# Six products of one tap instead of seven taps in five products, in a chain of filters on one Trainium2 core

## The chip, the cores and the metric

One core of one Trainium2 chip. TensorE (PE) multiplies, with its weight loads shown apart (PEld); VectorE (DVE), ScalarE (ACT) and GpSimd (POOL) work beside it; SyncE (SP) issues DMAs. The metric is device time of one launch in microseconds, here the median of three runs.

## The reference

The input x is 128 signals of 64 channels and 1024 samples, with a style vector of 128 numbers for each signal. Four convolution layers of three taps follow each other, and the result is added to x:

```python
s = style @ mw.T + mb
weight = SCALE * w * s[:, None, :, None]
demod = lax.rsqrt(jnp.sum(weight * weight, axis=(2, 3)) + EPS)
weight = weight * demod[:, :, None, None]
...
'same':       out = conv_same(x, weight) + b
'upsample':   out = blur(conv_up(x, weight) + b, 2 * [1, 3, 3, 1] / 8)
'downsample': out = conv_down(blur(x, [1, 3, 3, 1] / 8), weight) + b
...
x + layer3(layer2(layer1(layer0(x))))      # same, upsample, same, downsample
```

No nonlinear function stands between the layers, so the four of them are, for one signal, a single linear filter. The kernel forms that filter and applies it.

## The kernel before

Signals are taken four at a time, in 32 groups q. On the 128 partitions lie two halves of 64 channels (T and Bo), and every product of 64x64 is four matmuls, one for each quadrant of TensorE (`HALF` by `HALF`); the chip runs a float32 matmul as two records, so such a product is 8 records in the trace. For each group the filter is made in a chain:

- `scale3` copies the weights of layer 3, scaled by the group's factors, into two tiles wd (ACT, L399).
- Stage 1 multiplies them with the weights of layer 2. Polynomials of three taps each give one of five taps, p0 to p4, times -1 or 1. PSUM holds them in two banks, psS_0 and psS_1 (pool `ps_w`, which has one pair of banks), in blocks of 64 columns. They go to the tile S of eight blocks.
- Stage 2 (`stage2_rest`, L506) multiplies S with the blurred weights E of layer 1 and with differences of them (Ed, kept in the tile wsq) into psR, which is the same pair of banks as psS. For middle groups a part that two blocks share is made ahead (`share`, in free columns of a bank psA) and copied into psR by ACT (`share_copy`, L529). `share_sums` (DVE, L501) makes the two block sums that `share` reads.
- Stage 3 (L621) multiplies with the weights of layer 0, and the result Wf is the filter of nine taps. `combine_a` and `combine_b` (DVE, L712) make of it the weights H of a fast scheme with five products (`product`, L803) instead of more.

The input X is split in three planes, from which DVE and POOL make the inputs T of the five products (`in_g01` and `in_g2` on DVE, L712; `in04` on DVE, L790; `in3` on DVE, L761; `in1` and `in2` mostly on POOL, L776 and L781). `sum1` and `sum2` combine the products, ACT scales and shifts them into o (`output`, L880), and SP stores them.

The order is written out by hand. Each engine takes its instructions in the order of the code: `early_turn` for the first four groups, `turn_of` for those after, with side work of single turns in the table `SIDE` (the signals' ends: L1020, L1066, L1093, L1102, L1123, L1130 on DVE). A turn q does the convolution of group q, stage 3 of q + 2, and stage 1 of q + 4, for instance. Within `turn_of`, `stage1_a` stands behind stage 3 and the outputs of one phase; then come `copy_m3`, `in04`, `share_sums`, `in_g2`, the side work, the product `conv0` and two outputs, then `stage1_b`, `in_g01`, `share`, `share_copy`, outputs, and `conv1`. `stage2` opens the next turn.

Stage 1 has two forms. `stage1` does it undivided (groups 0, 1, 2 and 6). The other 28 groups use the form that needs seven tap products instead of nine, in two parts: `stage1_a` takes the taps' own products, negated, into PSUM, and ACT's L399 copies blocks 1 to 4 of each bank to S with the factor tBn; `stage1_b` adds two products of tap sums on top, and DVE's L481 reads PSUM times tB less p1. w3x and w2n hold the three taps and two sums of neighbouring taps (five blocks of 64). Last, POOL's L484 adds two blocks of S.

Of the kernel before, what the change touches and what calls it, by code (L numbers as in the profile page):

```python
# [48 lines left out]
F32 = mybir.dt.float32  # L49
AF = mybir.ActivationFunctionType  # L50
ALU = mybir.AluOpType
# [3 lines left out]
C = 64  # L55
K = 3
# [7 lines left out]
def kernel(  # L64
# [10 lines left out]
    NP, P, NXC = x.shape  # L75
# [7 lines left out]
    nc_v, nc_a, nc_g = nc.vector, nc.scalar, nc.gpsimd  # L83
# [45 lines left out]
    def weights(at):  # L129
        return par[:, at : at + KC].rearrange("i (k o) -> i k o", k=K)  # L130
# [3 lines left out]
    woi = {2: weights(cuts[1] + KC), 0: weights(cuts[3]), 1: weights(cuts[3] + KC)}  # L134
# [16 lines left out]
    E = const.tile([P, NT, C], F32, name="E")  # L151
# [160 lines left out]
    def var_newton(bs, ls=slice(0, NL)):  # L312
# [82 lines left out]
    chain = {}  # L395

    def scaled_copy(eng, dst, src, f):
        if eng is nc_a:
            nc_a.activation(dst, src, AF.Copy, scale=f)  # L399
        else:  # L400
            eng.tensor_scalar(dst, src, f, None, op0=ALU.mult)


    w3x = const.tile([P, 5, C], F32, name="w3x")
    w2n = const.tile([P, 5, C], F32, name="w2n")

    def split_weights():
        nc_g.tensor_copy(w3x[:, :K], w3)
        nc_g.tensor_scalar_mul(w2n[:, :K], woi[2], -1.0)
        for t, src in ((w3x, w3), (w2n, woi[2])):  # L410
            nc_g.tensor_add(t[:, K:], src[:, : K - 1], src[:, 1:])

    DIRECT = 3

    def scale3(q, engs=(nc_a, nc_a)):
        wd = []
        src = w3 if q < DIRECT else w3x
        n = src.shape[1]
        for j in range(2):
            t = wd_pool.tile([P, 5, C], F32, tag="wd", name=f"wd{q}_{j}")  # L420
            scaled_copy(engs[j], t[:, :n], src, tA[:, q, j : j + 1])
            wd.append(t)
        chain[q] = wd

    def tap_matmul(ps, wd, at, n, weight, taps, first=False, last=False):
        for r, rows in enumerate(HALF):
            for c, cols in enumerate(HALF):
                nc.tensor.matmul(  # L428
                    ps[r][cols, at * C : (at + n) * C],
                    weight[rows],  # L430
                    wd[c if r == 0 else 1 - c][rows, taps],
                    start=first,
                    stop=last,
                    skip_group_check=True,
                )
# [5 lines left out]
    def flat(t):  # L441
        return t.rearrange("c a o -> c (a o)")

    EVEN = slice(0, K, 2)

    def stage1(q, pool=None, engs=(nc_a, nc_a), between=None):

        wd = chain[q]
        ps = unit(pool or ps_w, f"psS{q}")
        for k, (at, at1) in enumerate(((0, 3), (3, 1), (1, 4))):  # L450
            tap_matmul(ps, wd, at, 2, woi[2][:, k, :], EVEN, first=k == 0)
            tap_matmul(ps, wd, at1, 1, woi[2][:, k, :], slice(1, 2), last=k == K - 1)
        if between:
            between()
        st, _ = s_tiles(q)
        for r in range(2):
            scaled_copy(engs[r], flat(st[r][:, 1:6]), ps[r][:, : 5 * C], tB[:, q, r : r + 1])
        chain[q] = st
        return ps

    def stage1_a(q, ps=None):

        ps = ps or unit(ps_w, f"psS{q}")
        wd = chain[q]
        tap_matmul(ps, wd, 2, 2, w2n[:, 0, :], EVEN, first=True)
        tap_matmul(ps, wd, 3, 2, w2n[:, 2, :], EVEN)
        tap_matmul(ps, wd, 1, 1, w2n[:, 1, :], slice(1, 2))
        st, t = s_tiles(q)
        for r in range(2):
            scaled_copy(nc_a, flat(st[r][:, :4]), ps[r][:, C : 5 * C], tBn[:, q, r : r + 1])  # L470
        chain[q] = wd, ps, st, t

    def stage1_b(q):

        wd, ps, st, t = chain[q]
        tap_matmul(ps, wd, 2, 1, w2n[:, 3, :], slice(3, 4))
        tap_matmul(ps, wd, 4, 1, w2n[:, 4, :], slice(4, 5), last=True)
        for r in range(2):
            p1 = st[r][:, 0:1, :].to_broadcast([P, 2, C])
            sums = ps[r][:, 2 * C : 6 * C].rearrange("c (a b o) -> c a b o", a=2, b=2)[:, :, 0]  # L480
            nc_v.scalar_tensor_tensor(  # L481
                st[r][:, 4:6, :], sums, tB[:, q, r : r + 1], p1, op0=ALU.mult, op1=ALU.subtract
            )
        nc_g.tensor_add(t[:, :, 2], t[:, :, 2], t[:, :, 0])  # L484
        chain[q] = st
        whole[q] = t

# [2 lines left out]
    Ed, Wd = later[:, :6], later[:, 6:8]  # L490
# [7 lines left out]

    def share_sums(q):
        t = whole[q]  # L500
        nc_v.tensor_add(t[:, :, 6:8], t[:, :, 1:5:3], t[:, :, 2:6:3])  # L501

    def chain_matmul(dst, weight, st, slots, last=False):
        for r, rows in enumerate(HALF):
            for c, cols in enumerate(HALF):
                nc.tensor.matmul(  # L506
                    dst[r][cols],
                    weight[rows],
                    st[c if r == 0 else 1 - c][rows, slots, :],
                    start=False,  # L510
                    stop=last,
                    skip_group_check=True,
                )

    def share(q, ps):

        at = [NB + 4 + i * C for i in range(3)]
        p12, p34 = ([b[:, i:j] for b in ps] for i, j in zip(at, at[1:]))
        chain_matmul(p12, E[:, 2], chain[q], slice(6, 7))
        chain_matmul(p34, E[:, 6], chain[q], slice(6, 7))  # L520
        chain_matmul(p34, E[:, 5], chain[q], slice(7, 8), True)
        shared_ps[q] = [b[:, at[0] : at[2]] for b in ps]

    def share_copy(q):
# [10 lines left out]
    def stage2_rest(q):  # L535

        ps = shared_ps.pop(q)
        block = lambda i, n=1: [b[:, i * C : (i + n) * C] for b in ps]
        apart = [b[:, : 4 * C].rearrange("c (a b o) -> c a b o", a=2, b=2)[:, :, 0] for b in ps]
        plan = (  # L540
            (apart, E[:, 0], slice(1, 4, 2)),
            (block(1), Ed[:, 0], slice(2, 3)),
            (block(2), Ed[:, 1], slice(1, 2)),
            (block(3), E[:, 2], slice(3, 4)),
            (block(3), Ed[:, 2], slice(2, 3)),
            (block(4), Ed[:, 3], slice(1, 2)),
            (block(4), E[:, 4], slice(3, 4)),
            (block(5, 2), E[:, 8], slice(2, 4)),
            (block(5), E[:, 6], slice(3, 4)),
            (block(1, 2), E[:, 1], slice(4, 6)),  # L550
            (block(2), E[:, 3], slice(4, 5)),
            (block(3), Ed[:, 4], slice(5, 6)),
            (block(4), Ed[:, 5], slice(4, 5)),
            (block(5), E[:, 7], slice(5, 6)),
        )
# [21 lines left out]
    def stage2_taps(q, taps, ps):  # L577

        st = chain[q]
        for n in taps:  # L580
            e = n - 2
            if e % 2 == 0:
                a, lo, m = slice(1, 4), e // 2 + 1, 3
            else:
                a, lo, m = slice(4, 6), (e + 3) // 2, 2
            for r, rows in enumerate(HALF):
                for c, cols in enumerate(HALF):
                    src = st[c if r == 0 else 1 - c]
                    nc.tensor.matmul(  # L589
                        ps[r][cols, lo * C : (lo + m) * C],  # L590
                        E[rows, e + 2, :],
                        src[rows, a, :],
                        start=(n == 0),
                        stop=(n == 8),
                        skip_group_check=True,
                    )
        return ps
# [573 lines left out]
    first = PART[0]  # L1171
# [210 lines left out]
    def early_turn(q):  # L1382
# [82 lines left out]
        if twice:  # L1465
            stage1_b(s)
# [93 lines left out]
    q, n, c = NQ - 3, NQ - 2, NQ - 1  # L1560
# [32 lines left out]
    q, n = NQ - 2, NQ - 1  # L1593
# [3 lines left out]
    o = opool.tile([P, 2, K, NB], F32, tag="o", name=f"o{n}")  # L1597
# [32 lines left out]
    for i in range(2):  # L1630
        plus(i, o[:, i, 1], psA, minus_td, y1[:, i])
        j = 1 - i
# [89 lines left out]
```

## Time and profile before

| | |
|---|---|
| time, median of 3 runs | 475.84 us (475.61 to 476.85) |
| span of the profiled execution | 475.5 us, from its first to its last instruction |
| mean granted TensorE clock | 0.998 |
| busy in the span | PE 469.7, DVE 417.3, ACT 312.0, POOL 165.8 us |
| stage 1 on PE, divided form | 1120 records; undivided 192 |
| longest waits | POOL L484 for ACT 139.6 us in 26 waits; POOL L776 for DVE 73.7 in 25 |

In a row of the timeline stand the start and the length in us, engine, line, operation, tiles written and read, shape and count; in brackets the idle time before it and what ended it. Rows of equal instructions are merged, so a length can cover several of them. In a row of groups the busy time in us and the mean of one in ns stand behind the bar, then the idle time before them. In a row of one tile's instructions stand least, median and greatest duration in ns.

### The profile page before, as it was taken

What the parts mean: (1) busy time and instruction counts of PE and PEld (TensorE: products, weight loads), DVE (VectorE), ACT (ScalarE), POOL (GpSimd) and SP (SyncE); (2) the same over time, 40 slices, a digit from 0 to 9 for tenths busy, and PEclk for the clock granted to TensorE, in tenths of its full rate; (3) what the DMA queues carried; (4) which work ended last, traced back from release to release, by engine and by line L of the source; (5) the groups of instructions that cost most, each with busy time, mean ns of one, the idle gap of its engine ahead of it and who ended that gap; (6) DMA issues with size and microseconds to landing.
All of it is one profiled execution on the core that took longest, in us unless ns stands there. A gap on an engine that the chain in (4) does not pass through costs nothing.

```text
span 475.5 us, 26771 instructions
## 1 busy us (share of the span) xinstructions
PE 469.7 (99%) x11932; PEld 349.5 (74%) x11932; DVE 417.3 (88%) x694; ACT 312.0 (66%) x711; POOL 165.8 (35%) x200
## 2 busy tenths in 40 slices
PE   9999999999999999999999999999999999999996
PEld 6987788777678876677776677766788787876653
DVE  3889998879989998899979899979998999999896
ACT  4565657577766676766667666667666777766464
POOL 3634033664444342233432233422333423243200
PEclk9999999999999999999999999999999999999999
DMA  5237456535445554345544454543555544455225
GB/s 176 71 115 224 150 151 180 152 113 177 139 145 166 166 166 136 123 150 169 163 150 126 130 168 152 178 124 121 152 164 169 164 145 147 148 152 161 80 91 193
DMA packets 52707, 70.71 MB, mean 149 GB/s; under 512 B 6000, under 2 KB 50672, under 8 KB 52592
## 3 DMA queue, kind: packets, MB, share of 16 engines
q1 hardware_dynamic: 52368, 68.78, 46.3%
q8 instruction: 93, 1.52, 1.4%
q10 hardware_dynamic: 224, 0.22, 0.1%
q14 instruction: 22, 0.18, 0.1%
HBM read 35.36 MB, written 33.62 MB: 145 GB/s over the span
## 4 chain that ended last, share of the span: by engine, by line
PE 99%; DVE 0%; ACT 0%; issue 0%
PE psA L803 47%; PE Y L803 12%; PE psR L506 9%; PE psW L621 7%; PE psA L621 7%; PE psS L428 6%; PE psR L589 5%; PE psA L506 2%; PE Y L1044 2%; PE Y L183 1%; PE Y L379 1%; PE psM L220 0%; PE psE L1044 0%; PE Y L255 0%; DVE o L882 0%; PE psM L255 0%
## 5 line engine op out<-in xcount | busy, mean ns | idle before, releaser
L803 PE MATMUL psA<-T,H 64*64 64x340 f32 x2304 | 185.9, 446 | 0.0
L803 PEld LDWEIGHTS psA<-T,H 64*64 64x64 f32 x2304 | 90.7, 133 | 46.9 <-issue 2.5
L712 DVE SCALAR_TENSOR_TENSOR G<-X 128x1376 f32<-128x1376 f32 (+2 forms) x65 | 78.0, 1206 | 0.2
L776 POOL TENSOR_TENSOR T<-G 128x684 f32<-128x684 f32 x28 | 46.3, 1652 | 73.7 <-DVE G L712 73.7
L484 POOL TENSOR_TENSOR S<-S 128x128 f32<-128x128 f32 x28 | 21.6, 772 | 139.7 <-ACT S L399 139.6
L399 ACT ACTIVATE R<-psR,tC 128x448 f32<-128x448 f32 x63 | 36.6, 631 | 43.6 <-PE psR L506 25.8
L803 PE MATMUL psA<-T,Wf 64*64 64x340 f32 x768 | 63.7, 446 | 0.0
L803 PE MATMUL Y<-T,Wf 64*64 64x340 f32 x768 | 62.4, 451 | 0.0
L712 DVE SCALAR_TENSOR_TENSOR Y<-m,psA 128x340 f32<-128x340 f32 x62 | 32.0, 516 | 28.2 <-PE psA L803 26.9
L399 ACT ACTIVATE psW<-psA 128x128 f32<-128x128 f32 x100 | 19.3, 268 | 49.1 <-PE psA L621 45.0
L790 DVE TENSOR_TENSOR T<-G 128x1368 f32<-128x1368 f32 (+1 forms) x33 | 50.8, 1541 | 0.0
L399 ACT ACTIVATE Wf<-psW,t 128x256 f32<-128x256 f32 (+2 forms) x76 | 32.7, 480 | 26.7 <-PE psW L621 26.4
L761 DVE TENSOR_TENSOR T<-X 128x684 f32<-128x684 f32 x32 | 47.7, 1492 | 0.0
L506 PE MATMUL psR<-S,E 64*64 64x64 f32 (+1 forms) x1472 | 46.8, 237 | 0.0
L781 POOL TENSOR_TENSOR T<-G 128x684 f32<-128x684 f32 x28 | 46.5, 1660 | 0.0
L428 PEld LDWEIGHTS psS<-wd,w2n 64*64 64x64 f32 x1120 | 35.1, 133 | 12.9 <-issue 0.3
L506 PEld LDWEIGHTS psR<-S,E 64*64 64x64 f32 x1472 | 39.5, 134 | 4.9 <-ACT psR L529 0.2
L803 PEld LDWEIGHTS Y<-T,Wf 64*64 64x64 f32 x768 | 30.3, 132 | 16.8
L803 PEld LDWEIGHTS psA<-T,Wf 64*64 64x64 f32 x768 | 29.8, 133 | 14.5
L880 ACT ACTIVATE o<-psA,tb,td 128x340 f32<-128x340 f32 x63 | 37.1, 648 | 5.0 <-PE psA L803 2.8
L880 ACT ACTIVATE o<-y,tb,td 128x340 f32<-128x340 f32 x62 | 38.5, 678 | 0.0
L880 ACT ACTIVATE o<-Y,tb,td 128x340 f32<-128x340 f32 x62 | 36.1, 639 | 2.8 <-PE Y L803 2.0
(180 smaller groups left out, 840.4 us busy)
## 6 DMA issues: line engine op xcount, KB each, us to landing
out<-o SPq DMA_DIRECT2D x191, 170.0 KB, 2.6
X<-in_x SPq DMA_DIRECT2D x150, 172.0 KB, 3.4
X<-in_x SPq DMA_DIRECT2D x14, 516.0 KB, 5.0
par<-in_params SPq DMA_DIRECT2D x3, 192.0 KB, 3.8
Xe<-in_x_ends SPq DMA_DIRECT2D x1, 512.0 KB, 4.5
out<-Oe SPq DMA_DIRECT2D x2, 96.0 KB, 2.1
out<-o ACTq DMA_DIRECT2D x1, 170.0 KB, 2.8
par<-in_params SPq DMA_DIRECT2D x1, 160.0 KB, 2.7
```

The costliest lines, as they stand in the source:

```text
L399: nc_a.activation(dst, src, AF.Copy, scale=f)
L428: nc.tensor.matmul(ps[r][cols, at * C : (at + n) * C], weight[rows], wd[c if r == 0 else 1 - c][rows, taps], start=first, stop=last, skip_ ...
L506: nc.tensor.matmul(dst[r][cols], weight[rows], st[c if r == 0 else 1 - c][rows, slots, :], start=False, stop=last, skip_group_check=True,)
L589: nc.tensor.matmul(ps[r][cols, lo * C : (lo + m) * C], E[rows, e + 2, :], src[rows, a, :], start=(n == 0), stop=(n == 8), skip_group_check ...
L621: nc.tensor.matmul(dst[r][cols], weight[rows], t[rows, c, slots, :], start=first, stop=last, skip_group_check=True,)
L712: nc_v.scalar_tensor_tensor(out, x, f, y, op0=ALU.mult, op1=op)
L761: nc_v.tensor_sub(t[:, pairs, 0, :NJ], plane(X, 3, pairs), plane(X, 1, pairs))
L776: eng.tensor_add(t[:, :, 0, :NJ], plane(g, 2), plane(g, 1))
L781: eng.tensor_sub(t[:, :, 1, :NJ], plane(g, 2), plane(g, 1))
L790: nc_v.tensor_sub(t[:, pairs, :, :NJ], both(a, PL), both(b, 1))
L803: nc.tensor.matmul(ps[s][cols, :NB], w, Ts[q, tag][rows, c, i, g : g + NB], start=(g == 0 and (m == 3 or alone)), stop=(g == K - 1), skip_ ...
L880: nc_a.activation(dst, src, AF.Identity, bias=add, scale=d3)
```

## The change

Stage 1 by six products of one tap each. w3x and w2n get a sixth block, the sum of the first and the last tap, and wd copies are 384 elements wide instead of 320. `stage1_a` puts each tap's own product in a block of its own (1, 3 and 4). ACT then makes four copies of 128 columns: blocks 1 and 3 of each bank to S's slots 0 and 4, and block 4 twice, to slots 5 and 7. POOL adds slots 0 and 4 into slot 6 and takes slot 5 from it, in `stage1_a` now. `stage1_b` adds three products of tap sums on top of blocks 1, 3 and 2, and DVE reads three blocks at once, times tB, less slots 5 to 7, into slots 1 to 3. S now holds p0 to p4 in slots 0 to 4, the sums of `share_sums` in 5 and 6. `stage2_rest` and `stage2_taps` read the same blocks at their new places. The undivided stage takes three taps at a time: three products of 192 columns instead of three of 128 and three of 64.

```diff
-            nc_g.tensor_add(t[:, K:], src[:, : K - 1], src[:, 1:])
+            nc_g.tensor_add(t[:, K : K + 2], src[:, : K - 1], src[:, 1:])
+            nc_g.tensor_add(t[:, K + 2], src[:, 0], src[:, 2])
...
 def stage1(q, ...):
-        for k, (at, at1) in enumerate(((0, 3), (3, 1), (1, 4))):
-            tap_matmul(ps, wd, at, 2, woi[2][:, k, :], EVEN, first=k == 0)
-            tap_matmul(ps, wd, at1, 1, woi[2][:, k, :], slice(1, 2), last=k == K - 1)
+        for k in range(K):
+            tap_matmul(ps, wd, k, K, woi[2][:, k, :], slice(0, K), first=k == 0, last=k == K - 1)
...
 def stage1_a(q, ps=None):
-        tap_matmul(ps, wd, 2, 2, w2n[:, 0, :], EVEN, first=True)
-        tap_matmul(ps, wd, 3, 2, w2n[:, 2, :], EVEN)
-        tap_matmul(ps, wd, 1, 1, w2n[:, 1, :], slice(1, 2))
+        for n, (i, at) in enumerate(((0, 1), (2, 3), (1, 4))):
+            tap_matmul(ps, wd, at, 1, w2n[:, i, :], slice(i, i + 1), first=n == 0)
         st, t = s_tiles(q)
         for r in range(2):
-            scaled_copy(nc_a, flat(st[r][:, :4]), ps[r][:, C : 5 * C], tBn[:, q, r : r + 1])
+            ends = ps[r][:, C : 5 * C].rearrange("c (a b o) -> c a b o", a=2, b=2)[:, :, 0]
+            scaled_copy(nc_a, st[r][:, 0:5:4, :], ends, tBn[:, q, r : r + 1])
+        for r in range(2):
+            middle = ps[r][:, None, 4 * C : 5 * C].to_broadcast([P, 2, C])
+            scaled_copy(nc_a, st[r][:, 5:8:2, :], middle, tBn[:, q, r : r + 1])
+        nc_g.tensor_add(t[:, :, 6], t[:, :, 0], t[:, :, 4])
+        nc_g.tensor_sub(t[:, :, 6], t[:, :, 6], t[:, :, 5])
...
 def stage1_b(q):
-        tap_matmul(ps, wd, 2, 1, w2n[:, 3, :], slice(3, 4))
-        tap_matmul(ps, wd, 4, 1, w2n[:, 4, :], slice(4, 5), last=True)
+        for n, (i, at) in enumerate(((3, 1), (4, 3), (5, 2))):
+            tap_matmul(ps, wd, at, 1, w2n[:, i, :], slice(i, i + 1), last=n == K - 1)
         for r in range(2):
-            p1 = st[r][:, 0:1, :].to_broadcast([P, 2, C])
-            sums = ps[r][:, 2 * C : 6 * C].rearrange("c (a b o) -> c a b o", a=2, b=2)[:, :, 0]
             nc_v.scalar_tensor_tensor(
-                st[r][:, 4:6, :], sums, tB[:, q, r : r + 1], p1, op0=ALU.mult, op1=ALU.subtract
+                flat(st[r][:, 1:4]),
+                ps[r][:, C : 4 * C],
+                tB[:, q, r : r + 1],
+                flat(st[r][:, 5:8]),
+                op0=ALU.mult,
+                op1=ALU.subtract,
             )
-        nc_g.tensor_add(t[:, :, 2], t[:, :, 2], t[:, :, 0])
...
 def share_sums(q):
-        nc_v.tensor_add(t[:, :, 6:8], t[:, :, 1:5:3], t[:, :, 2:6:3])
+        nc_v.tensor_add(t[:, :, 5:7], t[:, :, 0:2], t[:, :, 2:4])
```

What moves is seen in turn 23, where S27 is made. ACT's row of work from the copies of S27 on, before (tiles carry their group's number and a buffer number, psS27_0 and psS27_1 are the two banks):

```order
L399 ACTIVATE S27_7010<-psS27_0_6996,tBn_133 128x256
L399 ACTIVATE S27_7010<-psS27_1_6997,tBn_133 128x256
L842 COPY m3_24_7013<-psA24_6903 128x680
L880 ACTIVATE o23_6991<-y1_23_6811,tb_138,td_137 128x340 x2
L529 COPY psR26_0_7061<-psA23_6633 128x256
L529 COPY psR26_1_7062<-psA23_6633 128x256
```

The same place of ACT now:

```order
L399 ACTIVATE S27_7125<-psS27_0_7111,tBn_133 128x2x64
L399 ACTIVATE S27_7125<-psS27_1_7112,tBn_133 128x2x64
L399 ACTIVATE S27_7125<-psS27_0_7111,tBn_133 128x2x64
L399 ACTIVATE S27_7125<-psS27_1_7112,tBn_133 128x2x64
L847 COPY m3_24_7132<-psA24_7018 128x680
L885 ACTIVATE o23_7106<-y1_23_6926,tb_138,td_137 128x340 x2
L534 COPY psR26_0_7183<-psA23_6741 128x256
L534 COPY psR26_1_7184<-psA23_6741 128x256
```

Four copies stand where two stood; what follows has kept its order.

DVE at the same turn, from in04 to in_g01, before:

```order
L790 TENSOR_TENSOR T04_24_7015<-G24_6748 128x4x342
L501 TENSOR_TENSOR S26_6740<-S26_6740 128x2x128
L712 SCALAR_TENSOR_TENSOR G25_7018<-X1_106 128x2x342
L1130 TENSOR_TENSOR Ue1_163<-Ve1_165 128x64x9
L481 SCALAR_TENSOR_TENSOR S27_7010<-psS27_0_6996,tB_132,S27_7010 128x128
L481 SCALAR_TENSOR_TENSOR S27_7010<-psS27_1_6997,tB_132,S27_7010 128x128
L712 SCALAR_TENSOR_TENSOR G25_7018<-X1_106 128x2x688
```

and now:

```order
L795 TENSOR_TENSOR T04_24_7134<-G24_6860 128x4x342
L506 TENSOR_TENSOR S26_6848<-S26_6848 128x2x128
L717 SCALAR_TENSOR_TENSOR G25_7137<-X1_106 128x2x342
L1135 TENSOR_TENSOR Ue1_163<-Ve1_165 128x64x9
L482 SCALAR_TENSOR_TENSOR S27_7125<-psS27_0_7111,tB_132,S27_7125 128x192
L482 SCALAR_TENSOR_TENSOR S27_7125<-psS27_1_7112,tB_132,S27_7125 128x192
L717 SCALAR_TENSOR_TENSOR G25_7137<-X1_106 128x2x688
```

The order is the same and the two sums are half as wide again; they read slot 6 of S27, which POOL writes. POOL around it before, from the input sum of the turn ahead:

```order
L638 TENSOR_TENSOR R25_6877<-R25_6877 128x2x128
L781 TENSOR_TENSOR T12_24_6815<-G24_6748 128x2x342
L484 TENSOR_TENSOR S27_7010<-S27_7010 128x2x64
L776 TENSOR_TENSOR T12_25_7085<-G25_7018 128x2x342
L638 TENSOR_TENSOR R26_7147<-R26_7147 128x2x128
```

and now:

```order
L643 TENSOR_TENSOR R25_6992<-R25_6992 128x2x128
L786 TENSOR_TENSOR T12_24_6930<-G24_6860 128x2x342
L472 TENSOR_TENSOR S27_7125<-S27_7125 128x2x64
L473 TENSOR_TENSOR S27_7125<-S27_7125 128x2x64
L781 TENSOR_TENSOR T12_25_7207<-G25_7137 128x2x342
L643 TENSOR_TENSOR R26_7269<-R26_7269 128x2x128
```

POOL has two instructions in the place of one. The first is written in `stage1_a` now, which changes POOL's order only where side work of POOL stood between the two parts.

More of the change, by code (lines that the diff above doesn't have):

```diff
@@ L456, in stage1 @@
         for r in range(2):
[L457 removed]
+            scaled_copy(engs[r], flat(st[r][:, :5]), ps[r][:, : 5 * C], tB[:, q, r : r + 1])
         chain[q] = st
@@ L540, in stage2_rest @@
         plan = (
-            (apart, E[:, 0], slice(1, 4, 2)),
+            (apart, E[:, 0], slice(0, 5, 4)),
             (block(1), Ed[:, 0], slice(2, 3)),
-            (block(2), Ed[:, 1], slice(1, 2)),
-            (block(3), E[:, 2], slice(3, 4)),
+            (block(2), Ed[:, 1], slice(0, 1)),
+            (block(3), E[:, 2], slice(4, 5)),
             (block(3), Ed[:, 2], slice(2, 3)),
[L546 to L554, printed above, removed]
+            (block(4), Ed[:, 3], slice(0, 1)),
+            (block(4), E[:, 4], slice(4, 5)),
+            (block(5, 2), E[:, 8], slice(2, 5, 2)),
+            (block(5), E[:, 6], slice(4, 5)),
+            (block(1, 2), E[:, 1], slice(1, 4, 2)),
+            (block(2), E[:, 3], slice(1, 2)),
+            (block(3), Ed[:, 4], slice(3, 4)),
+            (block(4), Ed[:, 5], slice(1, 2)),
+            (block(5), E[:, 7], slice(3, 4)),
         )
```

17 lines of the change are left out of this document (8 added, 9 removed).

## The prediction

> **What bounds the kernel now.** I read the page first, its busy times and its chain.
>
> ```profile
> span 475.5 us, 26771 instructions
> PE 469.7 (99%) x11932; PEld 349.5 (74%) x11932; DVE 417.3 (88%) x694; ACT 312.0 (66%) x711; POOL 165.8 (35%) x200
> ...
> PE 99%; DVE 0%; ACT 0%; issue 0%
> ```
>
> PE is busy for 99% of the span and is 99% of the chain that ended last. PE time removed is therefore time gained, and every other cost counts only where it makes PE wait. The profiled span is 475.5 us against a median of 475.84, so 0.3 us lie around it; I make the sum on the span and add it to the median.
>
> Next the timeline of turn 23, one of the long middle turns (S27 is made here and psR26 is filled). PE rows, then the others:
>
> ```profile
> 369.25 0.73 PE L428 MATMUL psS<-wd,w2n 64*64 64x128 f32 x24
> 369.81 1.90 PE L803 MATMUL psA<-T,Wf 64*64 64x340 f32 x24
> 371.52 0.41 PE L428 MATMUL psS<-wd,w2n 64*64 64x64 f32 x16
> 371.75 0.53 PE L506 MATMUL psA<-S,E 64*64 64x64 f32 x24
> 372.10 1.90 PE L803 MATMUL psA<-T,H 64*64 64x340 f32 x24
> 373.82 0.40 PE L506 MATMUL psR<-S,E 64*64 64x128 f32 x8
> 374.04 0.41 PE L506 MATMUL psR<-S,wsq 64*64 64x64 f32 x16
> ```
>
> ```profile
> 370.02 0.84 ACT L399 ACTIVATE S<-psS,tBn 128x256 f32<-128x256 f32 x2 [0.32 <-PE psS L428]
> 370.23 0.42 DVE L501 TENSOR_TENSOR S<-S 128x256 f32<-128x256 f32 x1
> 370.57 0.86 DVE L712 SCALAR_TENSOR_TENSOR G<-X 128x684 f32<-128x684 f32 x1
> 370.94 0.81 POOL L484 TENSOR_TENSOR S<-S 128x128 f32<-128x128 f32 x1 [5.20 <-ACT S L399]
> 371.35 1.02 DVE L1130 TENSOR_TENSOR Ue<-Ve 128x576 f32<-128x576 f32 x1
> 372.29 0.59 DVE L481 SCALAR_TENSOR_TENSOR S<-psS,tB,S 128x128 f32<-128x128 f32 x2
> 372.72 0.63 ACT L529 COPY psR<-psA 128x256 f32<-128x256 f32 x2
> 372.81 1.57 DVE L712 SCALAR_TENSOR_TENSOR G<-X 128x1376 f32<-128x1376 f32 x1
> ```
>
> Starts on PE give the price of a product of four quadrants (8 records): 0.116 us for 64 columns (two from 371.52 to 371.75, three to 372.10) and 0.22 for 128 (373.82 to 374.04). Columns are paid, hardly anything per product. The second view gives the one chain that touches the change: stage1_b on PE, DVE's two L481, which empty the two banks of psS, ACT's two copies L529 into the same banks, then PE's psR at 373.82. The second copy ends at 373.35. With 0.06 for the signal (an estimate from the neighbouring hand-over, 370.86 to 370.94) PE is spared by 0.41 us.
>
> **The change, part by part.** PE: stage1_a goes from 0.56 (369.25 to 369.81) to three times 0.116, 0.35; stage1_b from 0.23 to 0.35. Together 0.79 becomes 0.70, 0.09 less in each of 28 turns: **-2.5 us**. The four undivided stages lose three products but no column:
>
> ```profile
> 82.63 1.19 PE L428 MATMUL psS<-wd,par 64*64 64x128 f32 x47
> ...
> 83.64 0.79 PE L803 MATMUL psA<-T,H 64*64 64x340 f32 x7
> ```
>
> ```profile
> 377.48 0.94 PE L621 MATMUL psA<-R,w0s 64*64 64x192 f32 x24
> 378.24 0.29 PE L621 MATMUL psA<-R,par 64*64 64x64 f32 x8
> ```
>
> The first took 1.01. The 24 records from 377.48 are one product of 192 columns and two of 128; 0.76 less 0.44 leaves 0.32, so three make 0.96: -0.05 each, **-0.2 us**.
>
> ACT: two copies of 256 become four of 128. The groups by shape bound one copy.
>
> ```profile
> L399 ACT ACTIVATE S<-psS,tBn 128x256 f32<-128x256 f32 x56 | 23.5, 471 | 11.6 <-PE psS L428 11.6
> L399 ACT ACTIVATE psW<-psA 128x128 f32<-128x128 f32 x100 | 19.3, 268 | 49.1 <-PE psA L621 45.0 <-issue 4.1
> L399 ACT ACTIVATE S<-psS,tB 128x320 f32<-128x320 f32 x7 | 3.4, 525 | 3.6 <-PE psS L428 3.6
> ```
>
> The slope from 256 to 320 is 0.054 for 64 elements, so 128 take 0.36; below stand the 0.27 of a copy with a constant factor, above the 0.47 itself. I take 0.37, with a new one every 0.27 (two of 256 fill 0.84, so the second starts 0.37 after the first, and 0.10 goes with the elements). Four fill 1.18, +0.34 a turn. In turn 23 they begin 0.21 earlier, at 369.81, since stage1_a is shorter; the end blocks are out at 370.45, the middle at 370.99, and the copies of L529 wait for DVE afterwards anyway. The wd copies of 384 instead of 320 elements add about 0.05 each, by the same slope, and ACT is busy for 66% of the span. Both cost nothing here as long as L529 waits for DVE and not for ACT.
>
> DVE: the two L481 take 192 instead of 128 elements.
>
> ```profile
> L481 DVE SCALAR_TENSOR_TENSOR S<-psS,tB,S x56: 274/339/351, 42.9 to 428.0; 128x128 f32<-128x128 f32 x56
> ```
>
> The first row shows 0.34 for 128. L712's time rises from 0.86 for 684 elements (at 370.57) to 1.57 for 1376 (at 372.81), which is 0.07 for 64. The pair ends 0.14 later. DVE itself catches up where it waits for PE, 26.9 us in 26 waits:
>
> ```profile
> DVE Y L712 <- PE psA L803: 26.9, 26, 1.9
> ```
>
> POOL: an add and a subtraction for one add, and now **DVE's L481 waits for the subtraction**, which it did not. This decides the sum. Alone, such an add takes 0.46:
>
> ```profile
> L484 POOL TENSOR_TENSOR S<-S x28: 455/821/1622, 40.6 to 426.5; 128x128 f32<-128x128 f32 x28
> ```
>
> In turn 23 it took 0.81: it ended at 371.75, 0.32 after DVE's L712 (two operands in SBUF) ended at 371.43; then L1130, issued at 371.35, took 1.02 for 576 elements and ended 0.62 after POOL. So the two engines take turns: one blocks the other, and who waits gets in when the other's instruction ends.
>
> The Trainium skill says the same (SBUF — State Buffer, section "SBUF: two separate sides"): a DVE operation with two SBUF inputs and a GpSimd operation share one port pair, whoever starts first holds it for the whole instruction, and the loser fully blocks. The rows agree, with 0.32 of work left after the block. By this rule the added subtraction is not free under DVE's work.
>
> After the change the add is ready at 370.53 (370.45 and the 0.08 of before). L501, also with two SBUF inputs, runs to 370.65, and L712 is issued at 370.57. A quiet add takes 0.46 of which 0.32 are left after a block, so it asks for its data some 0.14 after its start, at 370.67, behind L712. I take it that L712 goes first. Then the add ends at 371.75 as before, L1130 at 372.37, the subtraction 0.32 later at 372.69, and L481 starts at 372.77 instead of 372.29. The pair ends at 373.51, the second copy at 373.97, PE gets its banks at 374.03, but wants them at 373.73: **0.30 us of stall**, over three times the 0.09 gained.
>
> This holds where DVE has a two-input operation between L712 and L481: the extra work of turns 8, 9, 11 to 13, 16 to 18 and 20 to 27, sixteen turns. First and last of them:
>
> ```profile
> 153.15 0.38 PE L428 MATMUL psS<-wd,w2n 64*64 64x128 f32 x5
> 156.06 0.60 DVE L481 SCALAR_TENSOR_TENSOR S<-psS,tB,S 128x128 f32<-128x128 f32 x2
> ...
> 424.80 0.62 PE L428 MATMUL psS<-wd,w2n 64*64 64x128 f32 x16
> 427.69 0.60 DVE L481 SCALAR_TENSOR_TENSOR S<-psS,tB,S 128x128 f32<-128x128 f32 x2
> ```
>
> The pair ends 3.51 and 3.49 us after stage1_a's start in these, 3.63 in turn 23, and mostly between. Stalls run from 0.1 to 0.4; some operations are shorter or in pieces. I take 0.2 on average, **+3.2 us**. In the other middle turns DVE is free or PE has spare products in between, and the subtraction costs nothing.
>
> Early turns: there PE's psR waits for L481 directly, and DVE is late already.
>
> ```profile
> 42.87 0.60 DVE L481 SCALAR_TENSOR_TENSOR S<-psS,tB,S 128x128 f32<-128x128 f32 x2
> 43.35 0.55 PE L589 MATMUL psR<-S,E 64*64 64x192 f32 x6
> ...
> 57.33 0.60 DVE L481 SCALAR_TENSOR_TENSOR S<-psS,tB,S 128x128 f32<-128x128 f32 x2
> 57.82 1.09 PE L589 MATMUL psR<-S,E 64*64 64x192 f32 x22
> ...
> 100.74 0.14 DVE L1524 MEMSET Y<- 128x96 f32 x1 [2.39 <-ACT o L880]
> 100.79 0.53 DVE L481 SCALAR_TENSOR_TENSOR S<-psS,tB,S 128x128 f32<-128x128 f32 x2
> 101.02 0.38 PE L1295 MATMUL Y<-c0f,wsum 64*64 64x96 f32 x4
> ```
>
> In the first two the pair ends 0.12 after PE wanted psR, so +0.14 shows in full, with the 0.09 lost: 0.22 each. In turn 4 ACT's outputs stand behind the S copies and DVE's memset behind the outputs; +0.34 there and +0.14 are about 0.5. **+1.0 us** together.
>
> Sum: -2.5 - 0.2 + 3.2 + 1.0 = **+1.5 us**, or 477.3.
>
> **The rivals.** *The add gets in before L712.* Ready at 370.53 against 370.57, it does if the start decides or ACT's copies are a little shorter. Then L712, subtraction and L1130 follow in turn; L1130 ends 0.32 later, at 372.69, the pair 0.46 later (0.32 and 0.14) at 373.34, and PE waits 0.13 in turn 23, 0.1 on average: 16 times 0.1 is +1.6, and the sum -0.1: **475.7**, not slower. It decides from 0.05 us at the add's start. The port rule of the Trainium skill named above, taken by the word, gives this order.
>
> *PE's slack covers all.* If the subtraction runs beside L1130, or ACT and PE need less than I count between L481 and psR, only the products show, with about half of the early cost: **473.6**, faster. For it speaks that ACT waited for L481 only three times:
>
> ```profile
> ACT psR L529 <- DVE S L481: 1.0, 3, 0.6
> ```
>
> Against it, that L1130 and the add did exclude each other. It decides where the pair of L481 ends less than 0.32 later than now.
>
> *More turns stall.* If ACT's copies take 0.47 each (1.4 to 1.9 for four), the middle block comes late everywhere and all 23 turns from the fifth on lose 0.3: +6.9 - 2.7 + 1.0, **481.0**. The change not doing what it says is no rival: the products and their widths are given.
>
> **How the numbers follow.** Forecast 0.45, add first 0.25, covered 0.2, more stalls 0.1. About 0.3% (1.4 us) is what a measurement of this kernel can tell from no change. The forecast itself lies on that edge, so of its 0.45 some 0.30 is slower and 0.15 same; of the second 0.05 faster, 0.17 same, 0.03 slower; the third is faster, the last slower. Faster 0.25, same 0.32, slower 0.43. The range takes in most of the covered case and half a stall more per turn than forecast: 473.4 to 480.0.
>
> **What would show it.** PE starts 0.35 apart in both stages; POOL's add still ending 0.3 after L712, the subtraction 0.3 after L1130; L481 idle before it with POOL S as its releaser, some 0.4 in sixteen turns; PE's psR waiting for ACT's copy. If L1130 ends later instead, the add went first. If each turn is 0.09 shorter, the slack covered all. I am wrong most easily in the 0.32 us of slack in turn 23: 0.1 more or less over sixteen turns is 1.6 us.

## The result, and the profile after

The changed kernel takes **477.8 us** (median of 22 runs, 475.8 to 480.26), the kernel before 476.14 beside it (22 runs, 475.2 to 477.3). The ratio is 1.0033, with a 95% interval of 1.002 to 1.0047: about 1.6 us slower. One profiled execution of it has a span of 476.2 us and took 477.95 in all, so 1.75 us lie around a span.

First the page of the changed kernel, then its groups by shape.

```profile
span 476.2 us, 27139 instructions
PE 467.4 (98%) x12060; PEld 342.5 (72%) x12060; DVE 429.1 (90%) x694; ACT 323.9 (68%) x767; POOL 182.4 (38%) x230
...
PE 50%; DVE 2%; issue 0%; DVEq 0%
```

```profile
L399 ACT ACTIVATE S<-psS,tBn 128x128 f32<-128x128 f32 x112 | 32.0, 369 | 6.0 <-PE psS L429 3.3
L482 DVE SCALAR_TENSOR_TENSOR S<-psS,tB,S 128x192 f32<-128x192 f32 x56 | 20.4, 404 | 2.6 <-PE psS L429 1.4 <-POOL S L473 1.1
```

PE is busy for 2.3 us less than before (467.4 against 469.7), and yet the span is no shorter: PE waits now. The chain that ended last, 99% PE before, is PE for the last 50% of the span. Followed back it leaves PE at 234.66, and there, in order of time, it shows DVE:

```profile
231.07 0.85 DVE g L1021
...
231.94 1.68 DVE g L1021
233.62 0.44 DVE Y L717
```

So the largest single loss has a place: turn 13, and L1021 (L1016 before), the side work `setup1(1)`. To see the rest I cut both executions at the starts of `stage1_a`, which PE runs once in each turn 0 to 27. Each cell is the time from one such start to another, in us. The table also has two kernels of the experiments below, the old kernel with `setup1(1)` in another place and the changed one without GpSimd's two operations.

| stage | before | before, other place | after | after without GpSimd's sums |
|---|---|---|---|---|
| up to turn 0 | 38.46 | 37.92 | 36.96 | 37.44 |
| turns 0 to 4 | 72.77 | 72.63 | 73.61 | 74.18 |
| turns 5 to 12 | 113.15 | 113.19 | 112.44 | 112.32 |
| turns 13 and 14 | 29.41 | 29.77 | 31.38 | 29.23 |
| turns 15 to 26 | 171.02 | 171.25 | 171.40 | 169.88 |
| turn 27 to the end | 50.67 | 50.79 | 50.39 | 50.40 |

From turn 0 to turn 27 the changed kernel's execution takes 388.82 us, the old one's 386.34. The first row moves from execution to execution: over the fourteen profiles of this study, one of each kernel, it lies between 36.3 and 39.0, and both ends are kernels whose code is the changed kernel's up to that point. It says nothing of the change.

**Turn 23**, the one of the prediction, in the timeline of the changed kernel. It begins at 370.46, where it began at 369.25 before.

```profile
370.46 0.53 PE L429 MATMUL psS<-wd,w2n 64*64 64x64 f32 x24
370.81 1.90 PE L808 MATMUL psA<-T,Wf 64*64 64x340 f32 x24
371.02 1.14 ACT L399 ACTIVATE S<-psS,tBn 128x128 f32<-128x128 f32 x4
...
371.73 0.46 POOL L472 TENSOR_TENSOR S<-S 128x128 f32<-128x128 f32 x1 [4.81 <-ACT S L399]
371.77 1.14 DVE L717 SCALAR_TENSOR_TENSOR G<-X 128x684 f32<-128x684 f32 x1
372.31 0.92 POOL L473 TENSOR_TENSOR S<-S 128x128 f32<-128x128 f32 x1
372.52 0.53 PE L429 MATMUL psS<-wd,w2n 64*64 64x64 f32 x24
372.83 1.01 DVE L1135 TENSOR_TENSOR Ue<-Ve 128x576 f32<-128x576 f32 x1
372.87 0.53 PE L511 MATMUL psA<-S,E 64*64 64x64 f32 x24
...
373.77 0.73 DVE L482 SCALAR_TENSOR_TENSOR S<-psS,tB,S 128x192 f32<-128x192 f32 x2
374.26 0.63 ACT L534 COPY psR<-psA 128x256 f32<-128x256 f32 x2 [0.35 <-DVE S L482]
374.94 0.45 PE L511 MATMUL psR<-S,E 64*64 64x128 f32 x8
```

PE's part is as forecast: three products of 64 columns in 0.35 us, twice (370.46 to 370.81, 372.52 to 372.87). The four copies take 1.14. Then the order at the port: the add L472 starts 0.04 us before L717 and is quiet (0.46), and **L717 is the one that is held up**, 1.14 instead of 0.86. The subtraction L473 comes next and ends at 373.23, 0.32 after L717 (372.91). L1135 ends at 373.84, 0.61 after L473. DVE's pair ends at 374.50, 4.04 us after the turn's start, where it was 3.63 before.

One tile's instructions and who waited for them, S on DVE:

```profile
L482 DVE SCALAR_TENSOR_TENSOR S<-psS,tB,S x56: 340/405/418, 41.5 to 429.3; 128x192 f32<-128x192 f32 x56
...
  ACT psR L534: 5.6, 17
```

ACT's copies into psR waited for DVE's pair 3 times and 1.0 us before; now 17 times and 5.6 us. PE does not feel it in turn 23: ACT's second copy ends at 374.89, and PE's first product into psR starts at 374.94, 4.48 us into the turn, as it also does in the kernel without GpSimd's sums below.

S on POOL, over all 28 groups, and who waited for it:

```profile
L472 POOL TENSOR_TENSOR S<-S x28: 452/456/647, 39.1 to 427.0; 128x128 f32<-128x128 f32 x28
L473 POOL TENSOR_TENSOR S<-S x28: 456/919/967, 39.6 to 427.6; 128x128 f32<-128x128 f32 x28
...
  DVE S L482: 1.1, 3
```

The add is quiet nearly everywhere (0.456 in the median, 0.647 at most; the old form's add L484 had 0.821), so the order of turn 23 is no exception. DVE's pair waited for the subtraction in three turns.

**Turn 13**, DVE and POOL before (the turn begins at 224.37) and after (at 223.01):

```profile
231.98 0.74 DVE L1016 SCALAR_TENSOR_TENSOR g<-par,g 128x192 f32<-128x192 f32 x2
...
232.41 0.90 POOL L638 TENSOR_TENSOR R<-R 128x256 f32<-128x256 f32 x1 [1.08 <-ACT R L399]
232.84 1.07 DVE L712 SCALAR_TENSOR_TENSOR Y<-m,psA 128x340 f32<-128x340 f32 x2
233.26 1.64 POOL L781 TENSOR_TENSOR T<-G 128x684 f32<-128x684 f32 x1
```

```profile
230.96 0.74 POOL L643 TENSOR_TENSOR R<-R 128x256 f32<-128x256 f32 x1 [0.61 <-ACT R L399]
230.99 2.63 DVE L1021 SCALAR_TENSOR_TENSOR g<-par,g 128x192 f32<-128x192 f32 x2
231.64 1.76 POOL L786 TENSOR_TENSOR T<-G 128x684 f32<-128x684 f32 x1
...
233.54 1.05 DVE L717 SCALAR_TENSOR_TENSOR Y<-m,psA 128x340 f32<-128x340 f32 x2
...
234.66 1.95 PE L808 MATMUL Y<-T,Wf 64*64 64x340 f32 x24 [1.91 <-DVE Y L717]
```

Before, L1016 began 7.61 us into the turn, 0.43 before POOL's L638. Now the pair of stage 1 has pushed what follows on DVE by some 0.4, L1021 begins 7.98 into the turn, and POOL's L643 is there 0.03 earlier. The two operations of L1021 are let in one at a time, behind L643 and behind L786: 2.63 us instead of 0.74. sum2 (Y) comes late, and PE stands still for 1.91. The turn took 15.90 us instead of 13.84.

**Early turns**: turn 3 and turn 4 of the changed kernel, begun at 83.75 and 96.73.

```profile
84.34 0.86 DVE L717 SCALAR_TENSOR_TENSOR y<-psA,m 128x680 f32<-128x680 f32 x1
...
85.35 0.80 PE L808 MATMUL psA<-T,H 64*64 64x340 f32 x8 [0.36 <-DVE y L717]
...
97.60 1.15 ACT L399 ACTIVATE S<-psS,tBn 128x128 f32<-128x128 f32 x4
...
99.89 0.14 DVE L1529 MEMSET Y<- 128x96 f32 x1 [2.25 <-ACT o L885]
99.94 0.72 DVE L482 SCALAR_TENSOR_TENSOR S<-psS,tB,S 128x192 f32<-128x192 f32 x2
```

In turn 4 the memset stands 3.16 us into the turn instead of 2.86, behind ACT's four copies and two outputs, as forecast. In turn 3 DVE's sum1 is 0.33 later than before (0.59 into the turn instead of 0.26), and PE waits 0.36 for it.

### The profile page after: what moved, and what is told of

The parts are those of the page before. It is cut to its first block, busy times and chain, and to the rows that moved or that the text cites. A ratio compares the mean times of both kernels' runs of the same rounds, so it can differ in the third digit from the quotient of the medians.

```text
span 476.2 us, 27139 instructions
## 1 busy us (share of the span) xinstructions
PE 467.4 (98%) x12060; PEld 342.5 (72%) x12060; DVE 429.1 (90%) x694; ACT 323.9 (68%) x767; POOL 182.4 (38%) x230
## 4 chain that ended last, share of the span: by engine, by line
PE 50%; DVE 2%; issue 0%; DVEq 0%
PE psA L808 25%; PE Y L808 7%; PE psR L511 6%; PE psA L626 4%; PE psW L626 3%; PE psS L429 2%; PE Y L1049 1%; PE psA L511 1%; DVE g L1021 1%; PE psR L594 1%; DVE G L717 0%; DVE T L766 0%; PE psE L1049 0%; DVE Y L717 0%; DVE y L717 0%
## 5 line engine op out<-in xcount | busy, mean ns | idle before, releaser
L717 DVE SCALAR_TENSOR_TENSOR G<-X 128x1376 f32<-128x1376 f32 (+2 forms) x65 | 84.0, 1299 | 0.2
L472 POOL TENSOR_TENSOR S<-S 128x128 f32<-128x128 f32 x28 | 13.2, 472 | 135.6 <-ACT S L399 135.6
L717 DVE SCALAR_TENSOR_TENSOR Y<-m,psA 128x340 f32<-128x340 f32 x62 | 32.0, 516 | 21.2 <-PE psA L808 20.2
L786 POOL TENSOR_TENSOR T<-G 128x684 f32<-128x684 f32 x28 | 46.6, 1664 | 0.0
L511 PEld LDWEIGHTS psR<-S,E 64*64 64x64 f32 x1472 | 40.5, 134 | 5.2 <-ACT psR L534 1.0
L808 PEld LDWEIGHTS Y<-T,Wf 64*64 64x64 f32 x768 | 29.1, 132 | 20.2 <-DVE Y L717 2.1
L429 PEld LDWEIGHTS psS<-wd,w2n 64*64 64x64 f32 x1344 | 32.3, 134 | 13.0
```

Of the source, the lines that this page charges most:

```text
L429: nc.tensor.matmul(ps[r][cols, at * C : (at + n) * C], weight[rows], wd[c if r == 0 else 1 - c][rows, taps], start=first, stop=last, skip_ ...
L472: nc_g.tensor_add(t[:, :, 6], t[:, :, 0], t[:, :, 4])
L511: nc.tensor.matmul(dst[r][cols], weight[rows], st[c if r == 0 else 1 - c][rows, slots, :], start=False, stop=last, skip_group_check=True,)
L717: nc_v.scalar_tensor_tensor(out, x, f, y, op0=ALU.mult, op1=op)
L786: eng.tensor_sub(t[:, :, 1, :NJ], plane(g, 2), plane(g, 1))
L808: nc.tensor.matmul(ps[s][cols, :NB], w, Ts[q, tag][rows, c, i, g : g + NB], start=(g == 0 and (m == 3 or alone)), stop=(g == K - 1), skip_ ...
```

## The experiments

The theory after the result: three things cost time, each in its own place. (1) The early turns, 0.9 us. (2) GpSimd's sums ahead of the pair, which push DVE in the middle turns. (3) The collision in turn 13, which comes and goes. Against them the products save 0.09 a turn. The rivals: that the loss lies in only one of these, or that the products save less than their rows say. Ratios are to the kernel before on the same chip.

### The side work moved, in both kernels

```diff
-    LATE = {13: lambda: setup1(1)}
+    LATE = {}
...
+        14: lambda: setup1(1),
```

In the changed kernel:

> The changed kernel with one pair of VectorE's side instructions (the second half of setup1) moved from the end of turn 13 to the side work of turn 14, where TensorE has spare products. Theory A (one collision): in turn 13 this pair comes 0.37 us later than in the kernel before and is shut out by two GpSimd instructions, which costs 1.9 us of idle TensorE; without it the kernel is 1.5 to 2.0 us faster than the changed one, 476.0 us or about the time of the kernel before (ratio 0.999 to 1.001). Theory B (the forecast: 0.2 us of stall in each of sixteen turns): the pair counts for one turn only, 0.3 us at most, 477.5 us (ratio 1.002 to 1.004).

The same move in the old kernel, as control:

> The kernel before with the same pair moved in the same way, as a control. Its pair ran between two GpSimd instructions in turn 13 and TensorE waited for nothing there, so both theories expect no gain: 476.1 us, within 0.3 us (ratio 0.999 to 1.001). If it gains over 1 us, the pair was a cost of its own and the change has nothing to do with it.

The changed kernel: 477.34 us, ratio 1.0022 (1.0005 to 1.004), where theory B put it and not theory A. The old one: 475.92, 0.9999 (0.9983 to 1.0015). The move is free in the old kernel. In the changed one turn 13 is clean (13.83), but turn 14 takes 16.20 instead of 15.48, for its slot needs the result at once:

```profile
PE Y L1049 <- DVE g L1021: 0.5, 1, 0.5
```

So turn 13's loss in the profile is the collision, but this place has a loss of its own. The next kernel puts the pair into turn 7:

```diff
-        7: lambda: (small_rest(6), table_b(REST)),
+        7: lambda: (small_rest(6), table_b(REST), setup1(1)),
...
-    LATE = {13: lambda: setup1(1)}
+    LATE = {}
```

> The changed kernel with the same pair of VectorE's side instructions moved to turn 7 instead of turn 14 (in turn 14 TensorE's matmuls of the ends needed it at once). Theory A (one collision in turn 13): turn 13 takes 13.8 us instead of 15.9, turn 7 up to 0.3 more than 13.76, and the kernel is 1.0 to 1.9 us faster than the changed one (ratio 0.999 to 1.001). Theory B (stall spread over sixteen turns): 0.3 us at most (ratio 1.002 to 1.003).

476.76 us, ratio 1.003 (1.0017 to 1.0044). Turn 7 takes 14.03 instead of 13.75, turn 13 14.21. The time does not tell this from the changed kernel's 1.0033, and theory A's 0.999 to 1.001 is missed again. So in the changed kernel the collision of the profile is not the whole loss, and its mean cost is not settled by this run.

### Without GpSimd's two operations

```diff
-            middle = ps[r][:, None, 4 * C : 5 * C].to_broadcast([P, 2, C])
-            scaled_copy(nc_a, st[r][:, 5:8:2, :], middle, tBn[:, q, r : r + 1])
-        nc_g.tensor_add(t[:, :, 6], t[:, :, 0], t[:, :, 4])
-        nc_g.tensor_sub(t[:, :, 6], t[:, :, 6], t[:, :, 5])
+            middle = ps[r][:, None, 4 * C : 5 * C].to_broadcast([P, 3, C])
+            scaled_copy(nc_a, st[r][:, 5:8, :], middle, tBn[:, q, r : r + 1])
```

> The changed kernel without GpSimd's add and subtraction of stage 1: ScalarE writes the middle block to slots 5 to 7, so the middle tap's sum is left out and the filter of these groups is another one. Products, copies and VectorE's wider reads stay. Both theories expect TensorE's saving of 2.7 us less part of the early cost of 1.0: 473.4 to 474.5 us (ratio 0.994 to 0.997). Theory A expects the pair of turn 13 to be free of GpSimd again and turns of 13.75 us all through. If it stays above 475.5, neither GpSimd's sums nor the port are the cause, but the copies or the wider reads.

This kernel leaves out the middle tap's sum, so its filter is another one. 475.36 us, ratio 0.9992 (0.9977 to 1.0007): 2.0 us less than the changed kernel (about 1.0 to 2.9 with both intervals). **The loss of 1.6 us thus goes with GpSimd's two sums**; how it divides between turn 13 and the rest the times don't say. The middle turns are calm: the twenty turns 5 to 12 and 15 to 26 take 282.20 us, against 283.84 in the changed kernel (283.45 to 284.68 in the six other profiles with the sums ahead of the pair) and 284.17 and 284.44 in the two profiles of the old form. So the products save at most 2.0 to 2.2 us there, for the old form's one sum is missing here too, and GpSimd's sums give 1.6 of it back.

The 1.6 us are not spread. Turn by turn they lie mainly in turns 15 (15.80 instead of 15.40), 16 (13.94 for 13.75), 18 (14.33 for 13.81) and 20 (14.01 for 13.75), while turns 8, 9, 11, 12 and 23 differ by 0.03 at most. In turn 18 PE's psR starts late, 4.70 us into the turn instead of 4.48; what PE waited for in the other three is open.

The expected 0.994 to 0.997 was missed. What keeps the whole from being faster lies in the early turns, 74.18 us, where POOL's input sums move up and meet DVE:

```profile
84.13 1.30 DVE L980 TENSOR_SCALAR oc<-oc,par_s 128x16 f32<-128x16 f32 x1
```

L980 took 0.23 in the kernel before (as L977). sum1 stands behind it on DVE, and PE waits 1.2 us for sum1.

### The entry turn 4

Turn 4's first outputs ahead of ACT's copies of S:

```diff
         if entry:
             copy_m3(n)
+            outputs(q, 2)
             stage1_a(s)
-        outputs(q, 2)
         if not entry:
+            outputs(q, 2)
```

> The changed kernel with the order of ScalarE changed in turn 4 alone: the outputs stand ahead of the four copies of stage 1. The forecast put about 0.5 us there (VectorE's memset waits for the outputs, which wait for the copies); if that step is right, 0.4 to 0.6 us faster than the changed kernel, 477.3 us (ratio 1.002 to 1.003). If the cost of the early turns lies elsewhere, no difference: 477.8 (ratio 1.003).

477.93 us, ratio 1.0042 (1.0028 to 1.0057), no gain. Turn 4 takes 14.39 us instead of 13.84. The memset is early now, but PE's own next part waits for the copies:

```profile
98.05 1.15 ACT L399 ACTIVATE S<-psS,tBn 128x128 f32<-128x128 f32 x4
...
99.00 0.77 PE L429 MATMUL psS<-wd,w2n 64*64 64x64 f32 x22 [0.42 <-ACT S L399]
```

In either order PE waits for work of ACT's: for the memset behind ACT's outputs, or for the copies. Taking two of the four copies to DVE there, on top of the kernel with the setup in turn 7:

```diff
-            scaled_copy(nc_a, st[r][:, 5:8:2, :], middle, tBn[:, q, r : r + 1])
+            scaled_copy(nc_v if q == 8 else nc_a, st[r][:, 5:8:2, :], middle, tBn[:, q, r : r + 1])
```

> As e5_side7, and in turn 4 alone VectorE, which idles 2.2 us there before its memset, makes the two copies of the middle block in place of ScalarE. If ScalarE's two added copies are what delays the outputs, the memset and TensorE in turn 4 (the forecast's step, 0.5 us), turn 4 falls from 13.84 to about 13.4 us, and nothing else changes. If not, it stays at 13.8.

480.9 us, ratio 1.0113 (1.0093 to 1.0133). The turn takes 17.58 us. DVE takes its instructions in order, and all that stands behind the copies waits for ACT's first copies with them:

```profile
99.60 0.61 DVE L401 TENSOR_SCALAR S<-psS,tBn 128x128 f32<-128x128 f32 x2 [4.25 <-ACT S L399]
```

### The sums behind the pair

DVE subtracts p1, p0 and p1, as ACT copied them to slots 0 to 2, and GpSimd corrects p2 afterwards; S has p0 to p4 in slots 1, 3, 4, 5 and 7 (the setup in turn 7).

```diff
-        nc_g.tensor_add(t[:, :, 6], t[:, :, 0], t[:, :, 4])
-        nc_g.tensor_sub(t[:, :, 6], t[:, :, 6], t[:, :, 5])
...
-                flat(st[r][:, 1:4]),
+                flat(st[r][:, 3:6]),
...
-                flat(st[r][:, 5:8]),
+                flat(st[r][:, 0:3]),
...
+        nc_g.tensor_sub(t[:, :, 4], t[:, :, 4], t[:, :, 7])
+        nc_g.tensor_add(t[:, :, 4], t[:, :, 4], t[:, :, 0])
```

> As e5_side7, and the blocks of S lie so that VectorE's three-block read subtracts the middle block, the first end block and the middle block; GpSimd then corrects the middle sum (less the other end block, plus the middle) behind VectorE and no longer ahead of it, off every path to this turn's psR. GpSimd's instructions are as many as in the changed kernel. If the wait of VectorE for GpSimd and the order at the port is what costs, the middle turns fall to 13.75 us as they are without the sums, 1.6 us in all against e5_side7, and the kernel stands below the one before (ratio 0.995 to 0.998). If the sums cost by GpSimd's work as such, no gain against e5_side7.

482.93 us, ratio 1.0165 (1.0134 to 1.0195). Turns 13 and 14 take 29.23 us as without the sums, and the twenty middle turns 283.24. But in turns 0 and 1 stage 2 follows at once, and now it waits for GpSimd:

```profile
PE psR L594 <- POOL S L489: 4.1, 2, 2.5
```

The same with turn 4's two copies on DVE as well:

> e7_late_sums with the copies of turn 4 on VectorE as in e6_entry_dve: the version to which both steps point. Both gains together: 0.3 to 0.5 us below e7_late_sums, ratio 0.994 to 0.998 against the kernel before.

485.77 us, ratio 1.0229 (1.0196 to 1.0262): the losses nearly add.

### The old form for the early groups

The next four kernels keep the old form (products, slots, copies, one add behind the pair) for groups 0 to 8, and use the new one for groups 9 to 31.

```diff
+    NEW = 9
...
 def stage1_a(q, ps=None):
+        if q < NEW:
+            tap_matmul(ps, wd, 2, 2, w2n[:, 0, :], EVEN, first=True)
+            tap_matmul(ps, wd, 3, 2, w2n[:, 2, :], EVEN)
+            tap_matmul(ps, wd, 1, 1, w2n[:, 1, :], slice(1, 2))
...
+            return
```

They make a table of two by two: sums ahead of the pair or behind it, setup in turn 13 or 7. Sums ahead, setup in 13:

> The changed kernel, but groups 0 to 8, whose stage 1 lies in the early turns 0 to 4, keep the old form: old product list, old S slots, ScalarE's two copies 256 wide, one GpSimd sum, and no middle tap's sum ahead of the pair. Groups 9 to 27 have the new form as the change has it. Theory: the early turns cost the change about 0.9 us (73.61 us in the changed kernel's profile, 72.77 and 72.63 in two profiles of the old form). They come back to 72.5 to 73.0 us, the turns behind them stay as in the changed kernel (turns 15 to 26 at 171.4 us, turns 13 and 14 between 29.2 and 31.4 us), and the ratio to the kernel before falls from 1.0033 to about 1.0014 (1.000 to 1.003). Rival: the 0.9 us is the scatter of single profiles, and the loss lies in the middle turns alone: the ratio stays at 1.003 to 1.0045.

Sums behind, setup in 13:

> As the hybrid (groups 0 to 8 in the old form), and in groups 9 to 27 the sums of the middle tap lie behind the pair: VectorE's pair subtracts p1, p0, p1 as ScalarE copied them, and GpSimd then corrects p2 by -p4 + p1, in time for a stage 2 that comes a turn later. The setup of the side work stays in turn 13. Theory: two things ate the products' saving, the early turns and the sums ahead of the pair; without both, turns 5 to 12 and 15 to 26 run at the 112.3 to 112.8 and 169.9 to 170.5 us of the profiles without these sums or with late ones, the early turns at 72.7 us, and only turn 13 can still lose (0 to 2 us): ratio 0.9965 to 0.999, about 0.998. Rival: the products' 64 columns save less than the rows say once everything is in place, or the correction costs as much as the sums ahead did: ratio 1.000 or more.

Sums behind, setup in 7:

> As the hybrid with late sums, with the setup of the side work in turn 7 in place of turn 13. Theory: with turn 13's collision out of the way as well the kernel is 1.2 to 2.2 us faster than the kernel before, ratio 0.9955 to 0.9975; turns 13 and 14 together take 29.2 us, and turn 7 about 14.0 us. Rival: the pair in turn 7 loses as much as it did in turn 13 (0.3 us or more), and this is no better than the hybrid with late sums and the setup left in place; or, by the rival of that run, 1.000 or more.

Sums ahead, setup in 7:

> The hybrid (groups 0 to 8 in the old form, the rest as the change has it, GpSimd's sums ahead of the pair) with the setup of the side work in turn 7 in place of turn 13. Two single steps come out: against the changed kernel with the same setup in turn 7 (ratio 1.003) only the early turns differ, against the hybrid with the setup in turn 13 (ratio 1.005) only the setup's place. Theory: the early turns are worth about 0.9 us and turn 13's collision about 2, so that the ratio is 1.001 from both sides (1.000 to 1.0025), with turn 13 near 13.9 to 14.2 us and turns 0 to 4 near 72.6 us. Rival: the hybrid's 1.005 lies in the scatter of the middle turns, not in turn 13, and the early turns are covered elsewhere: the ratio stays at 1.003 to 1.005.

| | time, ratio (95%) | turns 0 to 4 | twenty middle turns | turn 13 |
|---|---|---|---|---|
| ahead, 13 | 478.1, 1.005 (1.0035 to 1.0065) | 72.46 | 283.87 | 16.04 |
| behind, 13 | 476.17, 1.0016 (1.0004 to 1.0027) | 72.82 | 283.18 | 14.60 |
| behind, 7 | 475.96, 1.0001 (0.9987 to 1.0014) | 73.10 | 283.53 | 13.85 |
| ahead, 7 | 476.48, 1.0007 (0.9993 to 1.002) | 72.39 | 284.68 | 14.02 |

In the profiles the early turns come back, to 72.4 to 73.1 us. The times don't settle what that is worth. With the setup in turn 7 the changed kernel has 1.003 and the hybrid 1.0007, so the early turns cost 0.0023 or 1.1 us (about 0.2 to 2 us with both intervals). With the setup in turn 13 the same step goes the other way, from 1.0033 to 1.005: the hybrid is 0.8 us slower (from 1.8 slower to 0.2 faster). If the collision in turn 13 struck the hybrid more often, that would explain it; this is not shown.

In the hybrid turn 13 shows clearly. With the sums ahead, the setup's place alone is worth 1.005 less 1.0007, 2.0 us (about 1.1 to 3.0), and the profile of the first has the collision again, 2.60 us for the setup pair where POOL came 0.05 earlier (PE's wait for sum2 behind it is 1.9 us):

```profile
231.80 0.73 POOL L675 TENSOR_TENSOR R<-R 128x256 f32<-128x256 f32 x1 [0.60 <-ACT R L399]
231.85 2.60 DVE L1053 SCALAR_TENSOR_TENSOR g<-par,g 128x192 f32<-128x192 f32 x2
```

What I expected of the sums behind, 1.2 to 2.2 us less than the kernel before, did not come: 1.0001 and 1.0016. The correction is not free either. Turn 18 takes 14.35 us there, as long as with the sums ahead (14.33), and 13.81 without GpSimd's operations. POOL and DVE of that turn, sums behind and setup in 13, which begins at 296.00:

```profile
300.28 1.74 POOL L513 TENSOR_TENSOR S<-S 128x128 f32<-128x128 f32 x1 [7.56 <-DVE S L505]
...
305.43 1.64 POOL L818 TENSOR_TENSOR T<-G 128x684 f32<-128x684 f32 x1
...
306.38 1.11 DVE L749 SCALAR_TENSOR_TENSOR H<-Wf 128x384 f32<-128x384 f32 x1
```

and the same place without GpSimd's operations, begun at 296.08:

```profile
304.71 1.64 POOL L784 TENSOR_TENSOR T<-G 128x684 f32<-128x684 f32 x1
...
306.26 0.55 DVE L715 SCALAR_TENSOR_TENSOR H<-Wf 128x384 f32<-128x384 f32 x1
```

L513 takes 1.74 beside a long DVE operation, where such a sum takes 0.46 when quiet. POOL's later sums slip by 0.8 (L818 begins 9.43 into the turn instead of 8.63), and the last of them, L818, shuts out DVE's first H (1.11 instead of 0.55), for which PE waits 0.2; the rest of the turn's loss is not traced. No version of this study beats the kernel before by more than its interval.

## Why the prediction was right in the sum, and where it was wrong

- **PE, -2.5 and -0.2: right.** Three products take 0.35 in both stages. A calm turn takes 13.75 instead of 13.84, 1.8 in twenty; without any GpSimd sum the twenty middle turns save 2.0 to 2.2. The undivided product of 192 columns came out as forecast too (0.97, from 81.06 to 82.03, against 0.96).
- **ACT, 0.37 a copy, free in the middle: right** (0.369, four in 1.14). The wd copies grew by 0.05 each (1.13 for two against 1.03). In turn 4, where I had counted them, PE's waits go back to ACT in both orders.
- **DVE, +0.14 for the pair: right** (0.404 each against 0.34 in the median before).
- **The order at the port: wrong.** The step that failed is "I take it that L712 goes first". The add starts first, at 371.73 against 371.77, and L717 is held up, as in my first rival, whose times fit: there the pair ends 4.09 us after the turn's start, here 4.04; forecast was 4.26. The sign that I had named for that order, L1130 (now L1135) ending later, is there: 0.61 after the subtraction. The rule of the Trainium skill (SBUF — State Buffer, section "SBUF: two separate sides"), that whoever starts first holds the port pair for the whole instruction, gave this order; the trace agrees, 0.46 for the add and 1.14 for L717. I had let an estimate of when the add asks for its data (0.14 after its start) overrule it.
- **Middle turns, +3.2: wrong in size and mostly in place.** I forecast a stall of 0.1 to 0.4 for psR in each of sixteen turns, 0.30 in turn 23. ACT's waits for DVE's pair came, in 17 turns, but turn 23 has no stall at psR, and DVE waited for the subtraction in three turns, not in sixteen. Without GpSimd's sums the twenty turns are 1.6 us shorter, mainly in four of them, of which turn 15 is none of the sixteen. That the rival's 16 times 0.1 also makes 1.6 is luck. (My 0.06 for the signal is 0.08 by the rows I took it from; this moves no term by more than 0.02.)
- **Turn 13: not foreseen.** I let a later DVE cost only where stage 1's own pair is waited for. DVE's later work in the same turn slips by 0.37 too, and there another pair stood 0.43 ahead of a POOL operation. It cost 2.06 in the profile. In the hybrid the setup's place was worth about 2.0 by the times; in the changed kernel its mean is open (0.1 us, at most about 1, by the time of the kernel with the setup in 7; 2.06 by the profile), and executions differ: turn 13 took 15.90, and 14.29 in the kernel that differs only in turn 4.
- **Early turns, +1.0: right in size by the profiles** (0.84 to 0.98); the times leave it open (1.1 with the setup in turn 7, the other sign with it in 13). Turns 0 and 4 lost as said (0.28 for 0.22, 0.50 for 0.5). Turn 1 lost 0.1 or nothing instead of 0.22, turn 3 lost 0.45 through sum1, which I had not named, and turn 2 gained 0.2 to 0.5.
- **The base.** I put 0.3 us around the span; 1.75 lie there. The old kernel's profiled execution took some 477.2 (an estimate, 475.5 and 1.75), 1.1 above the median, and the start before turn 0 alone moves by 2.6 us.

So the forecast, 477.3 against 477.8, was right by luck: two errors cancel, 1.6 us too much for the stalls of the middle, and nothing for turn 13. The rival's sum without turn 13 (475.7) would have been too low.

## What to carry to other kernels

Work that is off the critical path is not free when it holds a port that a busy engine needs: 64 columns less on TensorE in each group were worth about 2 us in the middle turns of the profiles, and two small GpSimd sums took 1.6 of them back there. When an engine slips by a few tenths, look through the whole turn for the place where it now comes just behind another engine's operation, not only at the wait of the edited line. A profile's order of two starts 0.04 us apart is no basis for a forecast with one order; give both orders their price.

## What the runs showed of the hardware

In turn 13 two GpSimd operations in a row let DVE in only between them: the pair L1021, 0.74 us in the kernel before, took 2.63 behind L643 and L786, L643 having started 0.03 us earlier; in the hybrid it took 2.60. Four ACT copies of 128 columns with a factor for each partition take 0.369 each, and copies of the same size into psW, from another source and without such a factor, 0.268. A GpSimd sum of 128 elements took 0.46 when quiet and 0.92 behind DVE in turn 23, with 0.32 left after the block. The first 37 us before turn 0 vary by 2.6 us between executions of kernels that are the same up to there; why is open.
